# Ranking messages two double blocks of sources at a time in a two-layer graph network, with a fixed room per pair, places turned in the second layer, more gathers ahead and another order of the first loads

## The chip, the cores and the metric

The kernel runs on one core of a Trainium2 chip. The metric is device time in microseconds (us), the median of the runs shown. Engines: TensorE (PE) does matrix products and transposes, VectorE (DVE) element work, scans and reductions, ScalarE (ACT) activations and copies, GpSimd (POOL) here mostly issues indirect transfers, and SyncE (SP) issues plain transfers. ACT and POOL issue some plain transfers too.

## The reference

A graph with 6250 nodes of 128 features and 106250 edges, sorted by destination: each of 50000 random pairs in both directions, and a loop at every node. Every edge has one of four types and 64 attributes. Two layers, each behind a layernorm and a ReLU, each added to its input:

```
h = relu(layernorm(x))
x = x + layer0(h)
h = relu(layernorm(x))
x = x + layer1(h)
return x
```

`layer0` is an attention over edges for each type (8 heads of 16 channels): a logit from a score of the source and one of the destination, a softmax over the edges of the same destination and type, and the weighted sum of the source's transformed features. The four sums of a node go through a GELU and a matrix, and a second attention mixes them with the node's own features.

`layer1` takes each edge in both directions, passes (features of one end, features of the other end, attributes) through 320x256 weights, a leaky ReLU and 256x128 weights, and adds the result to the node at the end. So every edge gives one message to its destination and one to its source. A node network follows.

```
src_full = concatenate([src, dst]); dst_full = concatenate([dst, src])
msg = leaky_relu(concatenate([nf[src_full], nf[dst_full], ef_full]) @ We1) @ We2
red = segment_sum(msg, dst_full, num_segments=N)
out = leaky_relu(concatenate([nf, red]) @ Wn1) @ Wn2
```

## The kernel before

**Tiling.** 63 destinations are a block (`GB`), 126 a double block or unit (`DB`): 100 blocks (`NBK`) and 50 units (`NU`). The edges of a block lie one behind the other; each block gets 9 tiles (`TB`) of 128 edges, starting at its first edge (`st0`). So there are 900 tile columns (`NT`). In another layout, used for work over all edges at once, edge number 832 p + j is element j of partition p (`J` = 832).

**Preparation (L193 to L433).** SP loads `src`, `dst`, types and the next destination of each edge. ACT issues 22 loads of `x` (L220, L222), then those of the weights (L230 to L241). `scores` (L238) forms attention scores from weights. The block starts are found (L291 to L336), and with them SP issues 100 loads of pieces of `e2` (source and type in one number, and destination) as rows into ten `ct` tiles (L347). Then a loop over the 50 units (L352) normalizes, transposes and multiplies, and stores for each node and type a row of the table `xt`, through POOL (L377), and its own terms through ACT (L374). Behind it ten turns (L384 to L393) transpose the `ct` tiles into index columns (`xi`, `dloc`), and a chain of eight steps makes `srci`, `inb` and `key` (L394 to L402). `skey` (L419 to L429) is the unit of each edge's source, in the layout of 832.

**First layer (L438 to L860).** 25 steps (`NS`) of four blocks, nine tiles each. A tile's `gather0` issues four indirect gathers of `xt` rows on POOL (the helper `gather`, L81) into one of 18 `xg` buffers, 17 tiles (`LA0`) ahead of its use. `masks`, `logits` and `soft` (four scans of 1152 columns with one operand in PSUM) belong to the next step and are spread over the tiles of the present one; `messages` (L581) multiplies gathered rows by the weights and sums them by PE; `nodes` (L621) finishes the step before and stores the table `abtab`, from which the second layer reads.

**The ranks.** The second layer writes each message for a source to DRAM (`m2d`) at a place, so that messages for the same source lie together. Edges are cut into five parts (`NPT`) of 27 partitions of the 832-layout; within a part the messages are ordered by the unit of the source. `count` (L718) compares `skey` with one unit number and sums, for each partition; 50 counts are called over the first four steps (`NCS`). `counted` (L723) sums them across partitions into starts (`base1`, and `st1` for the readers). `rank` (L760), 50 times, three a step from step 4 on, compares again, scans the 832 columns into running places, and copies those of the unit into `plc` by a predicated copy:

```
ts_(ind, skey, float(b), None, op0=ALU.is_equal)
scan(place, ind, zrow, base1[:, b:b + 1], op0=ALU.add, op1=ALU.add)
nc.vector.copy_predicated(plc, ind, place)
```

`plc` is stored to DRAM (L746), read back block by block by `place_load` (L774, 100 small loads on SP in the last steps), and transposed into the index columns `placei` by `place_turn` (L781). Edges that aren't a block's own get a place in a trash area behind the messages (`trash`).

**Second layer (L914 to L1075).** For each of 450 tile pairs: `gather_pair` (two indirect gathers of `abtab` rows on POOL, 3 pairs ahead, `AHEAD`, with `AHEAD + 2` buffers `ag`), two products into `z` (L1046), the sum with the gathered rows into `s` (L1048, DVE), a multiplication by 0.01 (L1049, ACT) and a maximum (L1050, DVE), then two indirect scatters to `m2d` at `placei` (L1054, POOL), and two products that add the destination's messages (L1064). `ready(u)` (L987) loads a unit's attributes, destinations and `rhs` rows through SP and makes its left sides. `windows(j)` (L935) reads back part j of `m2d` in 50 windows, at starts from `st1` (L942), and sums by source (L963, L964), beside the tiles of a later part; the last part's windows come behind all tiles, with `node_update` (L872).

**Order.** Each engine runs its instructions in the order in which the program's scheduler put them, which starts from the order of the calls; waits between engines come from the tiles and buffers. At the end, a counter of exceptions (`oddi`) decides whether a general path does all again; with these inputs it doesn't run.

Of the kernel before, what the change touches and what calls it, by code (L numbers as in the profile page):

```python
# [56 lines left out]
LA0 = 17  # L57
NCS = 4
# [16 lines left out]
MW = HID + 1  # L75
TRASH = 64 * P
AHEAD = 3
# [8 lines left out]
def kernel(ctx: ExitStack, tc: tile.TileContext, x, src, dst, ef, et, w_rel, a_src, a_dst,  # L86
# [27 lines left out]
    m2d = dram("m2d", (E + TRASH, MW))  # L114
# [69 lines left out]
    zrow = p0.tile([P, J], F32, name="zrow")  # L184
    base1 = p0.tile([P, NU], F32, name="base1")
# [4 lines left out]
    pcol = p0.tile([P, 3], F32, name="pcol")  # L190
    cnt = p0.tile([P, NU], F32, name="cnt")

    with ExitStack() as prep:  # L193
        cpool = prep.enter_context(tc.tile_pool(name="prep", bufs=1))
        wpool = prep.enter_context(tc.tile_pool(name="prep2", bufs=2))
        pp = prep.enter_context(tc.tile_pool(name="prepp", bufs=2, space=PSUM))

# [15 lines left out]
        for u0 in range(0, NU, 10):  # L213
            nc.gpsimd.memset(x_sb[:, u0:u0 + 10, :], 0.0)
            for q in range(2):
                n0 = u0 * DB + q * GB
                k = 10 if u0 + 10 < NU else 9
                xq = x[u0 * DB:(u0 + k) * DB, :].rearrange("(u q r) c -> q r u c", q=2, r=GB)[q]
                for r0, r1 in ((0, 48), (48, GB)):
                    nc.scalar.dma_start(x_sb[q * 64 + r0:q * 64 + r1, u0:u0 + k, :], xq[r0:r1])  # L220
        for h, n in halves(NU - 1):
            nc.scalar.dma_start(x_sb[h, NU - 1, :], x[n, :])  # L222


        wall = cpool.tile([P, R * XR + R * H + C + 2 * H], F32, name="wall")
        wx = wall[:, 0:R * XR].rearrange("p (r c) -> p r c", r=R)
        wd = wall[:, R * XR:R * XR + R * H].rearrange("p (r h) -> p r h", r=R)
        wso = wall[:, R * XR + R * H:]
        wr = cpool.tile([P, R, C], F32, name="wr")
        nc.scalar.dma_start(wr, w_rel.rearrange("r i o -> i r o"))  # L230
        nc.scalar.dma_start(wso[:, 0:C], w_self)
        nc.scalar.dma_start(wcx[:, 0:C], w_cross)
        nc.scalar.dma_start(brT, b_rel.rearrange("r c -> c r"))
        blb = cpool.tile([P, C], F32, name="blb")
        nc.scalar.dma_start(blb, b_l.partition_broadcast(P))
        tmp = cpool.tile([P, R * C], F32, name="tmp")

        def scores(o, w, a, r):  # L238

            ab = wpool.tile([P, R * C], F32, name="ab")  # L240
            nc.scalar.dma_start(ab[:, 0:r * C], a.partition_broadcast(P))  # L241
            tt(tmp[:, 0:r * C].rearrange("p (r c) -> p r c", r=r), w,
               ab[:, 0:r * C].rearrange("p (r c) -> p r c", r=r), op=ALU.mult)
            red(o, tmp[:, 0:r * C].rearrange("p (r h d) -> p r h d", r=r, d=D), axis=AX.X, op=ALU.add)

        nc.gpsimd.tensor_copy(wx[:, :, 0:C], wr)
        scores(wx[:, :, C:XR], wr, a_src.rearrange("r h d -> (r h d)"), R)
        scores(wd, wr, a_dst.rearrange("r h d -> (r h d)"), R)
        ws1 = wso[:, 0:C].rearrange("p (r c) -> p r c", r=1)
        scores(wso[:, C:C + H].unsqueeze(1), ws1, a_src_l.rearrange("h d -> (h d)"), 1)  # L250
        scores(wso[:, C + H:C + 2 * H].unsqueeze(1), ws1, a_dst_l.rearrange("h d -> (h d)"), 1)
        wc1 = wcx[:, 0:C].rearrange("p (r c) -> p r c", r=1)
        scores(wcx[:, C:C + H].unsqueeze(1), wc1, a_src_l.rearrange("h d -> (h d)"), 1)
# [97 lines left out]

        for u in range(NU):  # L352
            if u % 10 == 0:
# [9 lines left out]
            w = R * XR // 2  # L363
            for k in range(2):
                nc.tensor.matmul(ps[:, k, 0:w], hT, wall[:, k * w:(k + 1) * w], start=True, stop=True)
            nc.vector.tensor_copy(row.rearrange("p (a c) -> p a c", a=2), ps[:, :, 0:w])
# [14 lines left out]
        first = cpool.tile([P, NBK, TB], F32, name="first")  # L381
        nc.gpsimd.iota(first, [[GB, NBK], [0, TB]], base=0, channel_multiplier=0, allow_small_or_imprecise_dtypes=True)
# [1279 lines left out]
```

## Time and profile before

| | |
|---|---|
| median of 3 runs | 4176.27 us (4169.11, 4176.27, 4177.46) |
| the profiled execution | 4172.47 us, span from first to last instruction 4170.7 us |
| mean granted TensorE clock | 0.86 |
| PE matmul busy | 3111.7 us, 75% of the span, 11258 instructions |
| PE weight load busy | 1790.3 us, 43% |
| DVE busy | 2830.8 us, 68%, 5244 instructions |
| ACT busy | 1574.8 us, 38%, 2994 instructions |
| POOL busy | 2899.4 us, 70%, 2887 instructions |
| DMA | 754.26 MB, mean 181 GB/s |

How to read the lines that follow. A line of the costliest groups has the source line, engine, operation and tiles, the count, then busy us and mean ns of one, then the idle us of the engine just ahead of them and what ended most of it ("issue": nothing that the profile shows). A windows line has a stretch of the span, its length, and the busy us of each engine in it with the number of instructions, then the granted clock, the share of DMA time and GB/s. A timeline line has the start in us from the span's start, the duration, the engine (with a q: its issue of a transfer, with the time until it landed), line, operation and tiles, and in brackets the wait before it and what ended it. The gathers of both layers have line 81, that of the helper; they are told apart by the tiles `xg` and `ag`.

### The profile page before, as it was taken

To read this page: it belongs to the slowest core of one execution; us is meant where nothing else is said; L and a number is where in the kernel's file an instruction comes from. 1 tells how busy PE (TensorE), PEld (TensorE's weight loads), DVE (VectorE), ACT (ScalarE), POOL (GpSimd) and SP (SyncE) were. 2 spreads that over 40 slices of the span, in tenths; PEclk is the share of its full clock that TensorE was granted. 3 is DMA by queue.
4 is the path that set the end of the run, shared out by engine and by line. 5 is a ranking of instruction groups with operands and counts; after the bars stand their busy time and mean duration, and the time that the engine had idled before them with its cause. 6 is when DMAs were issued, how large, how long until landed. Compare 5 with 4: busy or idle time off the path is not lost. (4 is left out here: it accounts for less than half of the span.)

```text
span 4170.7 us, 43560 instructions
## 1 busy us (share of the span) xinstructions
PE 3111.7 (75%) x11258; PEld 1790.3 (43%) x11258; DVE 2830.8 (68%) x5244; ACT 1574.8 (38%) x2994; POOL 2899.4 (70%) x2887
## 2 busy tenths in 40 slices
PE   4558877777888855666678887688768787688888
PEld 3346555555666642222234443344324333244456
DVE  6767899999777744455556665566657666577755
ACT  2356666656666532222222332222222222222211
POOL 5777777777777506777777777777777777777700
PEclk9768878888888868788889898888989989899999
DMA  6645444445555417666578886788868888588754
GB/s 180 168 102 120 113 113 114 114 112 119 118 119 122 105 41 202 175 180 184 165 212 247 252 253 197 227 249 240 246 197 265 242 237 251 170 263 274 242 164 139
DMA packets 414703, 754.26 MB, mean 181 GB/s; under 512 B 182863, under 2 KB 249525, under 8 KB 414445
## 3 DMA queue, kind: packets, MB, share of 16 engines
q0 software_dynamic: 148800, 430.91, 35.6%
q1 hardware_dynamic: 230376, 288.41, 26.6%
q10 hardware_dynamic: 35268, 32.07, 2.7%
q8 instruction: 92, 1.51, 0.2%
q14 instruction: 167, 1.36, 0.1%
HBM read 586.43 MB, written 164.69 MB: 180 GB/s over the span
## 5 line engine op out<-in xcount | busy, mean ns | idle before, releaser
L81 POOL DMA_INDIRECT xg<-xt,xi x900 | 980.5, 1089 | 289.0 <-issue 237.8
L81 POOL DMA_INDIRECT ag<-abtab,srci x900 | 907.4, 1008 | 303.4 <-issue 203.0
L1054 POOL DMA_INDIRECT m2d<-s,placei x900 | 913.9, 1015 | 288.6 <-issue 213.7
L1046 PE MATMUL z<-rhs,lt 128*128 128x512 f32 x1800 | 1037.5, 703 | 0.6 <-ACT lt L1017 0.6
L1050 DVE TENSOR_TENSOR s<-s,z 128x1024 f32<-128x1024 f32 x450 | 548.3, 1220 | 560.9 <-ACT z L1049 559.1
L1064 PE MATMUL sums<-s,oh 128*64 128x256 f32 x1800 | 338.3, 459 | 486.5 <-DVE s L1050 485.5
L1048 DVE TENSOR_TENSOR s<-z,ag 128x1024 f32<-128x1024 f32 x450 | 549.5, 1221 | 189.5 <-PE z L1046 156.0
L1049 ACT ACTIVATE z<-s 128x1024 f32<-128x1024 f32 x450 | 461.0, 1024 | 389.1 <-DVE s L1048 388.6
L592 PE MATMUL acc<-oh,msg 128*128 128x256 f32 x1800 | 501.9, 421 | 71.1 <-DVE oh L591 51.4
L1046 PEld LDWEIGHTS z<-rhs,lt 128*128 128x128 f32 x1800 | 353.2, 216 | 449.3 <-issue 442.8
L1051 ACT COPY s<-srcf 128x2 f32<-128x2 f32 x450 | 86.9, 193 | 1207.4 <-DMA m2d<-s,placei 1193.4
L964 PE MATMUL sums<-mt,ohw 128*128 128x256 f32 x2024 | 528.1, 394 | 9.2 <-DVE ohw L963 9.2
L964 PEld LDWEIGHTS sums<-mt,ohw 128*128 128x128 f32 x2024 | 392.4, 200 | 202.8 <-issue 133.9
L592 PEld LDWEIGHTS acc<-oh,msg 128*128 128x128 f32 x1800 | 363.3, 212 | 164.3 <-DVE oh L591 74.0
L1064 PEld LDWEIGHTS sums<-s,oh 128*64 128x64 f32 x1800 | 98.8, 149 | 729.7 <-DVE s L1050 570.5
L591 DVE TENSOR_SCALAR oh<-iota,key 128x256 f32<-128x256 f32 x900 | 309.6, 365 | 93.0 <-PE acc L592 88.7
L599 ACT ACTIVATE junk<-dt,nthr 128x1152 bf16<-128x1152 f32 x250 | 313.8, 1255 | 17.2 <-DMA dt<-dtyp 12.3
L963 DVE TENSOR_SCALAR ohw<-col,at 128x128 f32<-128x128 f32 x1012 | 250.5, 299 | 19.5 <-PE sums L964 11.3
L584 DVE TENSOR_TENSOR msg<-xg,pt 128x512 f32<-128x512 f32 x225 | 148.6, 676 | 86.5 <-PE pt L577 81.3
L1013 PE MATMUL tp<-ident,fe 128*128 128x128 f32 x450 | 86.6, 299 | 138.1 <-ACT lt L1017 107.2
L1017 ACT COPY lt<-tp 64x384 f32<-64x384 f32 x300 | 141.7, 472 | 111.3 <-PE tp L1013 62.7
L1013 PEld LDWEIGHTS tp<-ident,fe 128*128 128x128 f32 x450 | 58.9, 151 | 212.3 <-ACT lt L1017 140.8
(276 smaller groups left out, 3467.0 us busy)
## 6 DMA issues: line engine op xcount, KB each, us to landing
mt<-m2d SPq DMA_DIRECT2D x156, 514.0 KB
db<-in_dst_dram SPq DMA_DIRECT2D x200, 288.0 KB
mt<-m2d SPq DMA_DIRECT2D x53, 642.5 KB
dt<-dtyp SPq DMA_DIRECT2D x100, 288.0 KB
fe<-in_edge_attr_dram SPq DMA_DIRECT2D x100, 288.0 KB
mt<-m2d SPq DMA_DIRECT2D x41, 385.5 KB
xg<-xt,xi POOLq DMA_INDIRECT x900
ag<-abtab,srci POOLq DMA_INDIRECT x900
```

What stands on the lines that cost most here:

```text
L81: nc.gpsimd.indirect_dma_start(out=o, out_offset=None, in_=table, in_offset=bass.IndirectOffsetOnAxis(ap=idx.bitcast(I32), axis=0))
L591: ts_(oh.rearrange("p t n -> p (t n)"), iota, key[:, k:k + 1], None, op0=ALU.is_equal)
L592: nc.tensor.matmul(acc[q // 2][:, :, q % 2, :], msg[:, q, :], oh, start=(i == 0 and q % 2 == 0), stop=(i == TB - 1), skip_group_check=True)
L599: nc.scalar.activation(junk, lanes[s]["dt"][v], AF.Sign, bias=nthr[:, u, t:t + 1], accum_out=g[:, v, t:t + 1])
L963: ts_(oh, col, at[:, i:i + 1], None, op0=ALU.is_equal)
L964: nc.tensor.matmul(sums, oh, mt[:, i, 0:HID], start=(i == 0), stop=(i == n - 1))
L1046: nc.tensor.matmul(z[:, q, :], lt[q][:, i * P:(i + 1) * P], rhs[(2 * u + q) % 4], start=True, stop=True)
L1048: tt(s[:, :, 0:2 * HID], z, ags.pop(n), op=ALU.add)
L1049: nc.scalar.mul(z, s[:, :, 0:2 * HID], 0.01)
L1050: tt(s[:, :, 0:2 * HID], s[:, :, 0:2 * HID], z, op=ALU.max)
L1054: st = nc.gpsimd.indirect_dma_start(out=m2d, out_offset=bass.IndirectOffsetOnAxis(ap=placei[:, k:k + 1], axis=0), in_=s[:, q, HID:HID + MW ...
L1064: nc.tensor.matmul(sums[q * 64:(q + 1) * 64, :], oh[:, q * TB + i, :], s[:, q, 0:HID], start=(i == 0), stop=(i == TB - 1))
```

## The change

- **Counts and ranks.** A scan serves two units, g standing for units 2g and 2g + 1. `skey` becomes the pair's number, and `sunit` (bf16) is 1 for the first unit and 2048 (`FIELD`) for the second. `count(g)` forms `own_` = (`skey` == g) * `sunit` with its sum, in one DVE instruction, 25 instead of 50; 14 (`NC0`) stand ahead of step 0, the others follow at the tiles of the first two steps, fixed in program order. `rank(g)`, 25 instead of 50, forms `own_` again, scans it with a starting value that holds two counters, 2048 apart, and copies under the predicate `own_`. `ranked()` behind the last rank takes the right field out and adds the pair's start.
- **Fixed room.** Each pair of a part has 1280 places (`ROOM`), so a pair's start doesn't depend on the pairs ahead of it; `m2d` gets `PLACES` = 160000 rows and the trash area. `counted` decodes the two counters, and tests that no pair exceeds its room.
- **Places in layer 2.** `place_load` and `place_turn` become `places(pool, bank, g)`, called in the second layer: group 0 ahead of `ready(0)`, the nine others at every fifth unit (loads at tile 1, turn at tile 8 of unit u with u % 5 == 2).
- **Gathers ahead.** `AHEAD` goes from 3 to 7, so `ag` has nine buffers for five.
- **First loads.** ACT issues the weights and attention vectors first, then the loads of `x` for units 0 to 19; those for the later units go to SP, behind the loads of `src`, `dst` and types. `scores` is formed right behind.
- **Columns and keys.** The ten column turns go into the last ten turns of the unit loop (`columns`), and the key chain moves behind the constants of the first layer. In `nodes`, one comparison (`va`) is fixed in program order.

```diff
+NC0 = 14
...
+FIELD = 2048.0
+ROOM = 1280.0
+PLACES = int(NPT * NU // 2 * ROOM)
...
-AHEAD = 3
+AHEAD = 7
...
-    m2d = dram("m2d", (E + TRASH, MW))
+    m2d = dram("m2d", (PLACES + TRASH, MW))
...
+        nc.scalar.dma_start(wr, w_rel.rearrange("r i o -> i r o"))
+        nc.scalar.dma_start(wso[:, 0:C], w_self)
+        nc.scalar.dma_start(wcx[:, 0:C], w_cross)
+        atts = []
+        for a in (a_src.rearrange("r h d -> (r h d)"), a_dst.rearrange("r h d -> (r h d)"),
+                  a_src_l.rearrange("h d -> (h d)"), a_dst_l.rearrange("h d -> (h d)")):
+            ab = cpool.tile([P, a.shape[0]], F32, name=f"ab{len(atts)}")
+            nc.scalar.dma_start(ab, a.partition_broadcast(P))
+            atts.append(ab)
+        def scores(o, w, ab, r):
+            tt(tmp[:, 0:r * C].rearrange("p (r c) -> p r c", r=r), w,
+               ab[:, 0:r * C].rearrange("p (r c) -> p r c", r=r), op=ALU.mult)
+            red(o, tmp[:, 0:r * C].rearrange("p (r h d) -> p r h d", r=r, d=D), axis=AX.X, op=ALU.add)
...
-                    nc.scalar.dma_start(x_sb[q * 64 + r0:q * 64 + r1, u0:u0 + k, :], xq[r0:r1])
+                    (nc.scalar if u0 < 20 else nc.sync).dma_start(x_sb[q * 64 + r0:q * 64 + r1, u0:u0 + k, :], xq[r0:r1])
...
+        def columns(g):
+            ct = cts[g]
+            ctf = wpool.tile([w, 2, P], F32, name="ctf")
+            nc.vector.tensor_copy(ctf, ct)
+            tp = pp.tile([P, 2, w], F32, name="tp")
+            for a in range(2):
+                nc.tensor.transpose(tp[:, a, :], ctf[:, a, :], ident[0:w, 0:w])
+            s = slice(g * w, (g + 1) * w)
+            nc.vector.tensor_copy(xi[:, s], tp[:, 0, :])
+            tt(dloc[:, s], tp[:, 1, :], first.rearrange("p b i -> p (b i)")[:, s], op=ALU.subtract)
         for u in range(NU):
+            if u >= NU - NBK // CG:
+                columns(u - NU + NBK // CG)
...
+        stt(rest, skey, -2.0 * DB, sf, op0=ALU.mult, op1=ALU.add)
+        ts_(rest, rest, float(DB), FIELD - 1.0, op0=ALU.is_ge, op1=ALU.mult)
+        ts_(sunit, rest, 1.0, None, op0=ALU.add)
...
+        ti = key.bitcast(I32)
...
-            tt(va, gt[:, :, 0:R].rearrange("p v t -> p t v"), gt[:, :, 1:R + 1].rearrange("p v t -> p t v"), op=ALU.is_gt)
+            c = tt(va, gt[:, :, 0:R].rearrange("p v t -> p t v"), gt[:, :, 1:R + 1].rearrange("p v t -> p t v"), op=ALU.is_gt)
+            tc.keep_in_program_order(c)
...
-        def count(b):
-            ind = wp.tile([P, J], U8, name="ind", bufs=1)
-            ts_(ind, skey, float(b), None, op0=ALU.is_equal, op1=ALU.add, accum_out=cnt[:, b:b + 1])
+        def count(g, pin=False):
+            own_ = wp.tile([P, J], F32, name="own_", bufs=1)
+            c = stt(own_, skey, float(g), sunit, op0=ALU.is_equal, op1=ALU.mult, accum_out=cnt2[:, g:g + 1])
+            if pin:
+                tc.keep_in_program_order(c)
...
+            ci = cp.tile([P, 2, NG], I32, name="ci")
+            nc.vector.tensor_copy(ci[:, 0, :], cnt2)
+            ts_(ci[:, 1, :], ci[:, 0, :], 11, None, op0=ALU.logical_shift_right)
+            ts_(ci[:, 0, :], ci[:, 0, :], int(FIELD) - 1, None, op0=ALU.bitwise_and)
+            nc.vector.tensor_copy(cnt, ci.rearrange("p t g -> p g t"))
...
+            tt(base1, before[:, :, 1], tots[:, :, 0], op=ALU.add)
+            stt(base1, base1, FIELD, before[:, :, 0], op0=ALU.mult, op1=ALU.add)
...
+            ts_(s1[:, :, 0], numb[:, 0:NG], ROOM, pcol[:, 1:2], op0=ALU.mult, op1=ALU.add)
...
-        def rank(b):
-            ind = wp.tile([P, J], U8, name="ind", bufs=1)
-            ts_(ind, skey, float(b), None, op0=ALU.is_equal)
+            ts_(odds, ps[:, 0:1], 0.0, None, op0=ALU.is_equal)
+            ts_(inb, inb, odds, None, op0=ALU.mult)
+        def rank(g):
+            own_ = wp.tile([P, J], F32, name="own_", bufs=1)
+            stt(own_, skey, float(g), sunit, op0=ALU.is_equal, op1=ALU.mult)
             place = wp.tile([P, J], F32, name="place", bufs=1)
-            scan(place, ind, zrow, base1[:, b:b + 1], op0=ALU.add, op1=ALU.add)
...
-        def place_load(g):
-            ct = wp.tile([CG * TB, P], F32, name="ctp", bufs=3)
-            regs = first_of(st0, g * CG, CG, E - CAP)
-            for k in range(CG):
-                nc.sync.dma_start(ct[k * TB:(k + 1) * TB], plcd[0, ds(regs[k], CAP)].rearrange("(i p) -> i p", p=P))
-            pcs[g] = ct
-        def place_turn(g):
-            w = CG * TB
-            s = slice(g * w, (g + 1) * w)
-            tp = pa.tile([P, 512], F32, name="ent")
-            nc.tensor.transpose(tp[:, 0:w], pcs.pop(g), ident[0:w, 0:w])
-            pf = wp.tile([P, w], F32, name="pf", bufs=1)
-            tt(pf, tp[:, 0:w], trash, op=ALU.subtract)
-            tt(pf, pf, inb[:, s], op=ALU.mult)
-            tt(placei[:, s], pf, trash, op=ALU.add)
+            scan(place, own_, own_, base1[:, g:g + 1], op0=ALU.add, op1=ALU.max)
+            nc.vector.copy_predicated(plc, own_.bitcast(I32), place)
+        def ranked():
+            lo = wp.tile([P, J], F32, name="place", bufs=1)
+            hi = wp.tile([P, J], F32, name="own_", bufs=1)
+            lo, hi, pi = lo.bitcast(I32), hi.bitcast(I32), plc.bitcast(I32)
+            nc.vector.tensor_copy(lo, plc)
+            ts_(hi, lo, 11, None, op0=ALU.logical_shift_right)
+            ts_(lo, lo, int(FIELD) - 1, None, op0=ALU.bitwise_and)
+            ts_(pi, sunit, 1.0, None, op0=ALU.is_gt)
+            nc.vector.copy_predicated(lo, pi, hi)
+            stt(plc, skey, ROOM, lo, op0=ALU.mult, op1=ALU.add)
+            ts_(plc, plc, pcol[:, 1:2], 0.0, op0=ALU.add, op1=ALU.max)
+            ts_(plc, plc, PLACES - 1.0, None, op0=ALU.min)
+            nc.sync.dma_start(plcd[0].rearrange("(p j) -> p j", j=J), plc)
+        rank_at = [(s, i) for s in range(NCS, NS) for i in ((0, 5) if s % 2 else (0,))]
...
+        for b in range(NC0):
+            count(b)
...
-                if s < NCS:
-                    for b in range(s * TB + i, NU, NCS * TB):
-                        count(b)
-                elif s == NCS and i == 0:
+                g = NC0 + s * TB + i
+                if g < NU // 2:
+                    count(g, True)
+                if (s, i) == (NCS, 0):
                     counted()
-                if s >= NCS and i % 3 == 0:
-                    b = (s - NCS) * 3 + i // 3
-                    if b < NU:
-                        rank(b)
-                    if b == NU - 1:
-                        nc.sync.dma_start(plcd[0].rearrange("(p j) -> p j", j=J), plc)
-                g = (s - NS + 1) * 3 + NBK // CG + (i - 3) // 2
-                if 0 <= g < NBK // CG and i in (3, 5, 7):
-                    place_load(g)
+                if (s, i) in rank_at[:NU // 2]:
+                    rank(rank_at.index((s, i)))
+                    if rank_at.index((s, i)) == NU // 2 - 1:
+                        ranked()
...
+        def places(pool, bank, g):
+            w = CG * TB
+            s = slice(g * w, (g + 1) * w)
+            ct = pool.tile([w, P], F32, name="ctp", bufs=1)
+            regs = first_of(st0, g * CG, CG, E - CAP)
+            for k in range(CG):
+                nc.sync.dma_start(ct[k * TB:(k + 1) * TB], plcd[0, ds(regs[k], CAP)].rearrange("(i p) -> i p", p=P))
+            yield
+            tp = bank()[:, 0:w]
+            nc.tensor.transpose(tp, ct, ident[0:w, 0:w])
+            pf = pool.tile([P, w], F32, name="pf", bufs=1)
+            tt(pf, tp, trash, op=ALU.subtract)
+            tt(pf, pf, inb[:, s], op=ALU.mult)
+            tt(placei[:, s], pf, trash, op=ALU.add)
...
             for n in range(AHEAD):
                 gather_pair(n)
+            for _ in places(wp, bank, 0):
+                pass
             for _ in ready(0):
                 pass
...
+                more = u % 5 == 2 and 2 * u + 6 < NBK
+                plcs = places(wp, bank, (2 * u + 6) // CG) if more else iter(())
...
+                    if i in (1, TB - 1):
+                        next(plcs, None)
```

## The prediction

> **What bounds the kernel now.** First the costliest groups of the page: three groups of indirect transfers on GpSimd (POOL), 900 each.
>
> ```profile
> L81 POOL DMA_INDIRECT xg<-xt,xi x900 | 980.5, 1089 | 289.0 <-issue 237.8
> L81 POOL DMA_INDIRECT ag<-abtab,srci x900 | 907.4, 1008 | 303.4 <-issue 203.0
> L1054 POOL DMA_INDIRECT m2d<-s,placei x900 | 913.9, 1015 | 288.6 <-issue 213.7
> ```
>
> The reader is to see that idle time before them is almost all "issue", about 0.3 us for each: POOL goes from one to the next. In layer 1 they run from 164.2 to 1433.4 us, in layer 2 from 1557.1 to 3970.2; only 164 us ahead, 124 between and 200 behind are not theirs. So a change counts where it starts POOL earlier, shortens its hole or quickens its pace.
>
> Second the windows of layer 1, cut where the ranks (L763 to L766) begin and end:
>
> ```profile
> core 0: us, PE busy (x) PEld busy (x) DVE busy (x) ACT busy (x) POOL busy (x), PEclk, DMA share, GB/s
> 164.10:451.20 287.10, 186.10 (x735) 127.43 (x736) 212.26 (x436) 152.68 (x273) 218.76 (x217) 0.71 0.51 117
> 451.20:1047.50 596.30, 465.94 (x1925) 329.08 (x1924) 555.27 (x1065) 369.00 (x660) 470.80 (x396) 0.82 0.48 112
> 1047.50:1434.00 386.50, 320.73 (x1365) 239.04 (x1364) 290.16 (x664) 257.14 (x465) 290.89 (x288) 0.84 0.50 118
> ```
>
> POOL's instructions here are the gathers: 287.1/217 = 1.32 us each, then 1.51, then 1.34. While ranks run, DVE is 93% busy and a gather costs 0.17 us more; 396 x 0.17 = 68 us is what ranking costs today. Third, the groups of DVE with what it consists of, and two rows of the timeline that show how:
>
> ```profile
> L765 DVE TENSOR_TENSOR_SCAN place<-ind,base,zrow 128x832 f32<-128x832 uint8 x50 | 97.2, 1944 | 0.6
> ...
> L766 DVE COPY_PREDICATED plc<-ind,place 128x832 f32<-128x832 uint8 x50 | 54.2, 1084 | 0.6
> L721 DVE TENSOR_SCALAR_CACHE_REDUCE ind<-skey 128x832 uint8<-128x832 f32 x50 | 50.9, 1018 | 1.3
> ...
> L763 DVE TENSOR_SCALAR ind<-skey 128x832 uint8<-128x832 f32 x50 | 30.1, 602 | 0.4
> ```
>
> ```profile
> 635.00 1.94 DVE L765 TENSOR_TENSOR_SCAN place<-ind,base,zrow 128x832 f32<-128x832 uint8 x1
> 635.21 2.49 POOL L81 DMA_INDIRECT xg<-xt,xi  x1 [0.31 <-issue]
> ```
>
> A gather that meets this scan takes 2.49 us; the median gather takes 0.952. Scans that read one operand from PSUM (L552 to L563, 2.54 us each) leave gathers at that median. So DVE work with two SBUF inputs costs POOL time: 68 us over 50 ranks is 1.36 us a rank, 0.45 us per us of its 3.03 us of two-input work (scan and predicated copy).
>
> Fourth, the timeline of the front:
>
> ```profile
> 10.56 30.17 ACTq L220 DMA_DIRECT2D x_sb<-in_x_dram  x16
> ...
> 47.86 1.27 ACT L148 ACTIVATE sq<-h_sb 128x1280 f32<-128x1280 f32 x1
> ...
> 59.70 0.71 DVE L366 COPY row<-ps 128x544 f32<-128x544 f32 x1
> ...
> 161.72 0.35 POOL L445 IOTA iota<- 128x256 f32 x1 [8.15 <-DVE key L400]
> ...
> 164.16 1.05 POOL L81 DMA_INDIRECT xg<-xt,xi  x1 [0.25 <-issue]
> ```
>
> ACT issues 22 loads of x before its first arithmetic; the first row follows at 59.7, the last at 151.4, and the first gather waits a further 13 us for columns and keys.
>
> **The change, part by part**, against the profiled execution: 4172.5 us (span 4170.7 and 1.8 around it), 3.8 under the median of 4176.3.
>
> Front. ACT keeps 8 of the 22 x loads, behind 8 weight loads: 8 x 1.61 to 1.89 and some 10 x 0.44 make it free at about 20 us. DVE is late next: its run of preparations ended at 36.9; the score instructions move into it (4.4 us by L242 and L244) and one memset leaves (0.75), so 40.5; reduction, reciprocal and product of the first layernorm add 3.2, and from there to the first row copy it took 3.3 before (56.4 to 59.7): 47 instead of 59.7. The 50 units keep their 91.7 us. The column turns took 7.1 us in a row (150.3 to 157.4); among the last ten units DVE has room (0.72 of 1.83 us a unit) but PE and the two tp banks are shared, so I book half, 3.5. In the new order four key instructions (2.2) stand ahead of the last row: 144.4, if the columns are there. SP is passed by 14 x loads (some 25 us), so e2's stores go from 19 to about 42, and the 100 column loads, queued also behind two late lacks stores (after six rows, 47 + 11), start near 60 instead of 36.6. They took 81 us (36.6 to 117.7; 0.81 each, group g after 8.1 more), so group 0 is there near 70 and group 9 near 143, while the unit loop wants them at 47 + 40 x 1.83 = 120 and 137. The cover of 50 us for group 0 is gone at group 8, and the last turn waits some 6 us; of that the 2.2 of key work may lie in the wait: last row near 148.5. Store, landing and small POOL work 5: first gather at 153.5, **-10**. Bounds: -18 if the loads go quicker with the x loads done, and +5 if they start at 75: every us that they slip, all gathers slip.
>
> Counts. Fifty at 1.02 (and 0.08 to read) ran from 166 to 221; the first softmax scan (221.85) waited for its ninth tile (es copied at 217.67), so removing 25 gains nothing. No row shows the new form (two inputs with a sum); the plain two-input one of 900 columns takes 1.09, which gives about 1.02 for 832. The old count read one SBUF input, the new one two: 25 x 1.02 x 0.45 = **+11.5**; bounds 0 (like L721) and 25.5 (POOL held throughout).
>
> The Trainium skill, "SBUF — State Buffer", section "Who interferes with whom", says that an accumulating tensor_scalar leaves GpSimd alone, while two SBUF inputs on DVE shut out a GpSimd instruction that reads SBUF for the whole instruction. The trace agrees in kind (the gather at 635.21) but the mean loss is 0.45 and not 1; by the rule taken whole, counts would cost 25.5 and ranks 101.
>
> Ranks. 25 instead of 50, each now a two-input compare (about 1.02 for 0.60), scan 1.94 and copy 1.08: 4.04 x 0.45 = 1.82 us each, 45.5 against 68: **-22.5**. Bounds: 1.36 each, -34; every us lost, 101, +33. The instruction order puts them between tiles 39 and 98, 3.8 a step, as dense as today's 4.2 and over half as long. The decoding afterwards (8 instructions, 6 us, two of them with two inputs) and the longer counted step (a dozen at 0.2): **+2**, bounds 0 and 8.
>
> End of layer 1. Thirty small DVE steps, ten transposes and 100 place loads go. From 1433 to 1557 the path is the last two steps' logits, scans, messages and nodes; DVE idled at each place step there. **-1** (0 to -4). The pinned compare waited 8.8 us once, with a scan 0.8 us behind it: 0.
>
> Start of layer 2:
>
> ```profile
> 1569.38 0.95 POOL L81 DMA_INDIRECT ag<-abtab,srci  x1 [0.30 <-issue]
> ...
> 1582.90 1.23 DVE L1048 TENSOR_TENSOR s<-z,ag 128x1024 f32<-128x1024 f32 x1 [3.91 <-PE z L1046]
> ...
> 1584.40 1.41 POOL L81 DMA_INDIRECT ag<-abtab,srci  x1 [14.07 <-DVE s L1048]
> ```
>
> POOL makes 10 gathers, then waits 14 us for the first add to free a buffer. With nine buffers it makes 18: 8 x 1.26 = 10 us of that is used. But ten place loads now stand first on SP, ahead of fe, db and rhs that the add needs: 11.78/20 = 0.59 each, 5.9 us. Net **-4**; +6 if more gathers in flight slow db's landing too (11 us already), -10 if the loads hide.
>
> Layer 2. Of 2413 us POOL really waits about 25 beyond its cadence. AHEAD moves the wait of a gather, but the scatter behind it in the same queue still waits for s: **-2** (0 to -14). Nine more place groups: 5.9 us of SP each, one transpose, three DVE steps of 0.25, per 240 us; SP's window loads are two windows early and hide them: **+1**, 10 without that cover. The tail keeps its 200 us.
>
> Sum: -10 + 11.5 - 22.5 + 2 - 1 - 4 - 2 + 1 = -25, so 4147.5 for the profiled execution, and 3.8 more beside the median: about **4151**.
>
> **Rivals.** (1) Slower: two-input DVE work holds POOL wholly. New two-input work is 25 x 1.02 + 25 x 4.04 + 2.1 = 129 us; at a loss of 1 it costs 129 instead of 68, less 16 of the other terms: +45, 4221. It decides from (68 + 16)/129 = 0.65 upward; 0.45 is measured, on ranks spread as densely. For it: the 2.49 us gather. Chance 0.14. (2) Only a part comes: column loads that start 10 us later still eat the front; -15, 4161. Chance 0.22. (3) No change: the pace is set by the message steps, which run 17 to 18 tiles behind the gathers, as far as buffers allow, and new waits in SP's queue eat the rest; 4176. Against it: these steps also took 54 us with ranks and 48 without. Chance 0.09. The forecast has 0.55.
>
> **The numbers.** 0.2% is 8.4 us, about what a measurement can tell from no change. Forecast and (2) lie below 4168: faster 0.77; (3) same 0.09; slower 0.14. The range goes from -62 (ranks -34, counts 0, front -18, layer 2 -10) at 4114 to 4178, which takes in (2) and (3).
>
> **What would show it.** First row near 47, the last column load near 143 and the first gather near 153 us; gathers at about 1.5 us for some seven steps instead of twelve, 1.34 after; layer 2's first hole near 10 us; gathers and scatters at 1.33 as now. Wrong: a first gather after 164, counts under which gathers take 1.6, or scatters that wait for placei.

## The result, and the profile after

The changed kernel takes 4135.4 us (median of 4 runs, 4131.7 to 4145.1) beside 4174.7 for the kernel before (4 runs): a ratio of 0.991, 95% interval 0.990 to 0.993. The forecast was 4151, in a range from 4114 to 4178. Sign and range held; the sum was 12 us too small in the profiled executions (25 forecast, 37.5 measured: 4172.5 to 4135.0), and it was not made of the terms that the forecast gave it. Runs 5 to 12 below were taken where every kernel, the one before too, took about 20% longer; their times are compared only within their own sets.

Columns of the table: us of the profiled executions. The stages are cut at the first and last gather or scatter of each layer on POOL:

| stage | before | after | change | forecast |
|---|---|---|---|---|
| until the first gather | 164.2 | 154.9 | -9.2 | -10 |
| gathers of layer 1, first to last | 1269.2 | 1263.0 | -6.2 | -9 |
| from there to the first gather of layer 2 | 123.8 | 99.1 | -24.7 | -1 |
| layer 2, first gather to last scatter | 2413.1 | 2416.3 | +3.2 | -5 |
| behind it | 200.5 | 200.0 | -0.5 | 0 |

The page of after, its groups of indirect transfers:

```profile
L85 POOL DMA_INDIRECT xg<-xt,xi x900 | 961.6, 1068 | 301.7 <-issue 244.2
L1104 POOL DMA_INDIRECT m2d<-s,placei x900 | 915.6, 1017 | 297.9 <-issue 217.4
L85 POOL DMA_INDIRECT ag<-abtab,srci x900 | 905.6, 1006 | 297.3 <-issue 204.6
```

Only the gathers of layer 1 became shorter (1089 to 1068 ns); the other two groups are as before. The windows of layer 1, with the ranks in the second (columns as in the windows of before):

```profile
154.90:391.00 236.10, 140.03 (x536) 93.87 (x536) 146.86 (x301) 117.30 (x206) 179.29 (x176) 0.70 0.51 116
391.00:826.30 435.30, 351.77 (x1432) 248.05 (x1431) 385.46 (x760) 270.02 (x489) 340.47 (x293) 0.82 0.47 112
826.30:1418.00 591.70, 494.07 (x2078) 364.80 (x2077) 436.62 (x986) 416.85 (x723) 441.87 (x432) 0.82 0.52 122
```

236.1/176 = 1.34 us for a gather with the counts, 435.3/293 = 1.49 with the ranks, and then 591.7/432 = 1.37, where the kernel before had 1.34. The second window takes in 60 us ahead of the first rank's scan, which starts at 451.6; from there on 249 gathers take 374.7 us, 1.50 each, for 396 at 1.51 before. So a gather beside the ranks costs what it did, and about seven steps of 36 gathers have it instead of eleven (forecast: seven for twelve); but the stretch behind the ranks became slower.

The front of after, three views put together (SP's, DVE's and POOL's rows of the timeline):

```profile
63.04 80.62 SPq L356 DMA_DIRECT2D ct<-e  x100
...
45.94 0.72 DVE L392 COPY row<-ps 128x544 f32<-128x544 f32 x1 [0.19 <-PE ps L391]
...
139.78 0.72 DVE L392 COPY row<-ps 128x544 f32<-128x544 f32 x1 [1.17 <-DMA xt<-row]
145.92 0.29 DVE L367 CAST ctf<-ct 90x256 f32<-90x256 int32 x1 [5.42 <-DMA ct<-e]
...
149.61 0.72 DVE L392 COPY row<-ps 128x544 f32<-128x544 f32 x1 [0.19 <-PE ps L391]
...
154.94 1.53 POOL L85 DMA_INDIRECT xg<-xt,xi  x1 [0.33 <-DMA t<-turnd]
```

The 13.8 us that the first row gains (59.7 to 45.9) are not all kept: the column loads on SP end at 143.7, DVE waits 5.4 us for the last of them, and the last row stands behind that turn.

The stretch between the layers. The timeline of before, PE's rows and then DVE's:

```profile
1453.20 5.78 PE L592 MATMUL acc<-oh,msg 128*128 128x256 f32 x26
1463.60 0.33 PE L521 MATMUL lg<-ne,pen 16*128 16x384 bf16 x1
...
1483.15 2.56 DVE L552 TENSOR_TENSOR_SCAN f<-km,l 128x1152 f32<-128x1152 f32 x1 [0.62 <-ACT l L534]
```

and of after:

```profile
1425.92 0.33 PE L535 MATMUL lg<-ne,pen 16*128 16x384 bf16 x1
1427.75 2.76 PE L606 MATMUL acc<-oh,msg 128*128 128x256 f32 x12
1430.99 1.03 PE L606 MATMUL acc<-oh,msg 128*128 128x256 f32 x4
1431.95 0.33 PE L535 MATMUL lg<-ne,pen 16*128 16x384 bf16 x1
...
1441.11 2.55 DVE L566 TENSOR_TENSOR_SCAN f<-km,l 128x1152 f32<-128x1152 f32 x1
```

`lg<-ne` opens a third of the logits of the last step, `acc<-oh,msg` are the products of the step before it. In the kernel before, the last step's logits stand on PE behind all products of step 23; in the changed kernel they stand among them, as in all earlier steps of both kernels. The first scan of the last step starts 72.1 us behind that of step 23 in the one (1411.06 to 1483.15) and 47.8 in the other (1393.36 to 1441.11).

The start of layer 2 in after, SP's, DVE's and POOL's rows:

```profile
1517.09 6.28 SPq L959 DMA_DIRECT2D ctp<-plcd  x8
...
1533.29 0.82 DVE L1051 TENSOR_SCALAR lt<-db,swap 64x1152 f32<-64x1152 int32 x1 [5.70 <-DMA db<-in_dst_dram]
1540.85 0.81 DVE L1051 TENSOR_SCALAR lt<-db,swap 64x1152 f32<-64x1152 int32 x1 [6.75 <-DMA db<-in_dst_dram]
...
1546.23 0.95 POOL L85 DMA_INDIRECT ag<-abtab,srci  x1 [5.71 <-DVE s L1098]
```

The 14.07 us hole is 5.7 us now, with 18 gathers ahead of it; the place loads go first on SP, and DVE waits for `db` behind them.

### The profile page after: what moved, and what is told of

The parts are those of the page before. It is cut to its first block, busy times and chain, and to the rows that moved or that the text cites. A ratio compares the mean times of both kernels' runs of the same rounds, so it can differ in the third digit from the quotient of the medians.

```text
span 4133.3 us, 43383 instructions
## 1 busy us (share of the span) xinstructions
PE 3116.2 (75%) x11258; PEld 1791.8 (43%) x11258; DVE 2739.6 (66%) x5139; ACT 1604.5 (39%) x3014; POOL 2883.5 (70%) x2887
## 3 DMA queue, kind: packets, MB, share of 16 engines
q0 software_dynamic: 148800, 430.91, 35.6%
q8 instruction: 92, 1.51, 0.2%
## 5 line engine op out<-in xcount | busy, mean ns | idle before, releaser
L85 POOL DMA_INDIRECT xg<-xt,xi x900 | 961.6, 1068 | 301.7 <-issue 244.2
L554 PE MATMUL km<-t,turn 8*128 8x512 bf16 x150 | 45.8, 421 | 136.3 <-DVE l L577 44.3
```

Source lines behind the costliest of these rows:

```text
L85: nc.gpsimd.indirect_dma_start(out=o, out_offset=None, in_=table, in_offset=bass.IndirectOffsetOnAxis(ap=idx.bitcast(I32), axis=0))
```

## The experiments

Each edit is shown against the changed kernel where nothing else is said, with "..." where lines are left out. Lane loads are the loads of a step's edges through SP (`loads(s)`: `t`, `db`, `ne`, `dt`), two steps ahead of their use; the gap is the time from the last gather of layer 1 to the first of layer 2.

Theories: **A**, the 24.7 us between the layers come from where the last step's logits stand in the instruction order. **B**, the place steps themselves cost them, by their waits. **C**, the comparison fixed in program order brought them. Of the slower pace behind the ranks, which the first two runs brought up: **D**, the order of DVE's instructions in the steady step; **E**, the removal of the places does it in another way.

**1. Places back in layer 1.** Places alone are undone; everything else stays changed.

```diff
+            yield
+            g = (s - NS) * 3 + NBK // CG
+            for k in range(3):
+                if 0 <= g + k < NBK // CG:
+                    place_turn(g + k)
...
+                g = (s - NS + 1) * 3 + NBK // CG + (i - 3) // 2
+                if 0 <= g < NBK // CG and i in (3, 5, 7):
+                    place_load(g)
                 if i == 5 and s + 2 < NS:
                     loads(s + 2)
...
-            for _ in places(wp, bank, 0):
-                pass
```

> The changed kernel, with the place loads and place turns back in the last steps of layer 1, at the places where the kernel before has them; all else stays changed. In the instruction order the logits of step 24 then stand behind all products of step 23 on PE, as before; in the changed kernel they stand among them. Theory A (order: the 24.7 us that the gap between the last gather of layer 1 and the first of layer 2 lost, 123.8 to 99.1, come from that order): the gap returns to about 124, messages of step 23 to 24 take 73 us instead of 48, and the time is about 4155 (25 more, less some 5 that the place loads no longer take at the start of layer 2). Theory B (the place steps themselves cost it, by their waits on DVE and PE): the same here. Theory C (the comparison fixed in program order brought it): the gap stays near 99, 4135.

**2. The same, with the place loads behind the lane loads** (against run 1).

```diff
-                g = (s - NS + 1) * 3 + NBK // CG + (i - 3) // 2
-                if 0 <= g < NBK // CG and i in (3, 5, 7):
-                    place_load(g)
                 if i == 5 and s + 2 < NS:
                     loads(s + 2)
+                g = (s - NS + 1) * 3 + NBK // CG + i - 6
+                if 0 <= g < NBK // CG and i >= 6:
+                    place_load(g)
```

> As the run before, but each step's place loads stand behind the lane loads of the step after next in the program (tiles 6, 7, 8 instead of 3, 5, 7). The same 100 loads and ten turns are in layer 1; in the instruction order the logits of step 24 are back among the products of step 23. Theory A (order): the gap is near 100 to 105 although all place steps are there, and the time 4130 to 4140. Theory B (the place steps themselves): the gap is 118 or more, about 4150. Theory C (the fixed comparison): 99 here too, and no difference from the run before.

**3. Without the fixed comparison.**

```diff
-            tc.keep_in_program_order(c)
```

> The changed kernel without the fixed program order of the comparison in the node steps. Theory A (order of the logits): the gap stays near 99, since the logits of step 24 stay where they are. Theory C: it grows by 9 or more, the wait for the tally that was seen before the first scan of the last step. Of the pace: message steps 12 to 23 took 49.3 us in the changed kernel and 48.4 in the rank-free steps before; if the fixed comparison costs that, they fall to 48.4 and the time by about 10, to 4125; if not, 4135.

**4. Three gathers ahead.**

```diff
-AHEAD = 7
+AHEAD = 3
```

> The changed kernel with AHEAD = 3 and five buffers, as before. Forecast's theory (the longer lead fills the hole at the start of layer 2 and costs nothing later): the first four units take 6 us longer (111.8 against 105.3 for 72 transfers of the kernel before and this one), so 4141. Rival (the lead is given back at the end: the last two units took 109.9 us with seven ahead and 101.4 with three, as only scatters are left there, which wait for sums): start 6 longer, end 8 shorter, so 4133, no difference that can be told.

Measured, beside runs of the kernel before on the same chip (its median 4182.6; the changed kernel beside 4174.7, from above). The last four columns are us of the profiled executions, the last of them from the first message product of step 23 to that of step 24:

| kernel | median | ratio, 95% interval | layer 1 | gap | layer 2 | messages of step 23 to 24 |
|---|---|---|---|---|---|---|
| after (from above) | 4135.4 | 0.9913 (0.9896 to 0.9929) | 1263.0 | 99.1 | 2416.3 | 47.9 |
| 1, places back | 4125.3 | 0.9871 (0.9852 to 0.9891) | 1241.3 | 116.0 | 2405.5 | 70.4 |
| 2, places back, loads late | 4114.7 | 0.9838 (0.9824 to 0.9852) | 1244.6 | 104.1 | 2408.1 | 49.3 |
| 3, comparison not fixed | 4145.1 | 0.9905 (0.9888 to 0.9923) | 1266.6 | 99.4 | 2423.2 | 45.8 |
| 4, AHEAD = 3 | 4134.8 | 0.9884 (0.9867 to 0.9901) | 1265.4 | 102.8 | 2411.8 | 48.8 |

Between the layers it counts where the place loads stand, and B, the place work itself, falls. Runs 1 and 2 do the same 100 loads and ten turns in layer 1 and differ in three lines; the gap is 116.0 and 104.1, and the step to the last one 70.4 and 49.3 us. Of the 21 us, run 1 gets 9 back behind that step (46.0 us from there to the first gather of layer 2, 54.7 in run 2), so its gap stays below the 124 that were expected, and 12 us of the gap are shown to hang on these lines. The places' own work is about the 5 us between run 2 and after. PE's first logits of the last step in run 1, and DVE's first scan behind them:

```profile
1414.33 5.34 PE L606 MATMUL acc<-oh,msg 128*128 128x256 f32 x24
1425.73 0.49 PE L535 MATMUL lg<-ne,pen 16*128 16x384 bf16 x1
...
1444.12 2.56 DVE L566 TENSOR_TENSOR_SCAN f<-km,l 128x1152 f32<-128x1152 f32 x1 [8.86 <-ACT l L548]
```

and the same scan in run 2, in its usual place:

```profile
1426.31 2.55 DVE L566 TENSOR_TENSOR_SCAN f<-km,l 128x1152 f32<-128x1152 f32 x1
```

SP in run 1 and then in run 2, the place loads `ctp` and the last `db` of the last step's lane loads:

```profile
1385.28 11.77 SPq L829 DMA_DIRECT2D ctp<-plcd  x20
...
1406.32 0.47 SPq L512 DMA_DIRECT2D db<-in_dst_dram  x1
```

```profile
1381.54 0.48 SPq L512 DMA_DIRECT2D db<-in_dst_dram  x1
...
1394.14 17.03 SPq L829 DMA_DIRECT2D ctp<-plcd  x30
```

So the change gained here not by moving work to layer 2 but because its place loads no longer stand on SP ahead of the last step's lane loads; the instruction order has the logits behind all products where they do. Whether that order alone cost the time, as A says, or loads that came late isn't separated: with the order the last `db` load moved too. It was issued 9.7 us behind the first product of step 23 in run 1 (1396.61) and 21.4 ahead of it in run 2 (1402.93); 8.6 behind it in the kernel before and 19.7 ahead in after. The first logits follow it by 13 to 19 us in all four, so most of their shift is already in the loads. C falls with run 3: the gap stays at 99.4 without the fixed comparison.

What nobody expected is the other column: with the places back, layer 1 takes 22 us less. POOL's own rows of the waits, from 880 to 1360 us, in after and then in run 2 (total, times, longest):

```profile
POOL xg L85 <- issue: 99.7, 278, 3.3
```

```profile
POOL xg L85 <- issue: 88.7, 291, 0.3
```

In run 2 POOL never waits longer than the 0.3 us between two gathers: the gathers set the pace (47.9 us a step is 36 x 1.33). In after it stops seven times, for 1.8 to 3.3 us, some 15 us in all; the profile names no releaser, and a free buffer is the likely one, since a message step takes 49.5 us on average of steps 12 to 22. The work of the step is the same in both. The order of DVE isn't. In short from the instruction order of step 17 (M message product, o one-hot, b m r statistics and root of the node step, F A L the scans and their products, h the normalized rows, T a mask; the first scan is the first F):

```
after:   ..bbmmomromrorMrorororrrorFhhAoFoTooooooALTF
run 2:   ..bbmomomromrMrororFrorArorFrohhoTAoLoooooTF
```

In after the first scan stands behind all ten r; in run 2 behind five of them. In step 17 it starts 25.7 us after the step's first message in after, and 24.5 in run 2; the last F, the share, starts at 42.2 and 41.0, and the next step's messages wait for it. Run 4, which has the order of after, has its pace (message steps 48.1 to 50.8 from 14 to 22); run 1 has the order of run 2 and a mean of 48.0 over steps 12 to 22. Run 3 alternates between two further orders, and between 48.5 and 50.4. The place of the first scan can't be all: it stands behind eight r in the kernel before from step 17 on, with steps of about 48.2 there, and behind eight in those steps of run 3 that take 50.4.

Run 4 also settles the gathers ahead. Counted by POOL's transfers, 36 a unit, the first four units take 207.8 us for 201.0 with seven, the last two 100.9 for 109.6. The end in after (waits on POOL from 3824 to 3935):

```profile
POOL m2d L1104 <- DVE s L1100: 12.1, 8, 2.8
...
POOL m2d L1104 <- DVE ohw L1006: 7.1, 7, 2.4
```

With seven ahead the last 20 transfers are scatters alone (12 with three), and they wait for sums, which DVE makes between the windows. What the start gains, the end gives back: no difference that the intervals can tell. The gain at the start is the lead itself: 82 of its 144 transfers are gathers, for 78 with three, and the 72nd scatter ends 224.5 us after the first gather with seven and 221.1 with three.

**5 to 8. The columns early; ranks twice; the kernel before with its loads late; five ahead.** In 5, the stores of `turnd`, `lacks` and `dtyp` go behind the column loads:

```diff
-            ne = wpool.tile([P, J], BF16, name="ne")
+            ne = cpool.tile([P, J], BF16, name=f"ne{r}")
...
             cts.append(ct)
+        for r in range(R):
+            nc.sync.dma_start(lacks[r].rearrange("(p j) -> p j", j=J), nes[r])
```

> The changed kernel with the stores of turnd, lacks and dtyp behind the 100 column loads on SP (four ne tiles instead of two, so that DVE needn't wait for them). Two effects are expected. Front: if the column loads set the end of the front (they ran from 63.0 to 143.7 and the last turn waited 5.4 us for them), they start near 39 and end near 120, the last turn doesn't wait, and the first gather is near 149 instead of 154.9; if the unit loop sets it, 154 to 155. Steps: in the instruction order of this kernel the steady steps of layer 1 have the order of DVE that the run with the places back had (first scan behind the second group of the node steps' small instructions), not that of the changed kernel (behind all of them, and behind two h). Theory D (the order of the steady step costs 1.5 us a step: message steps 12 to 22 took 49.5 us in the changed kernel and 47.9 with the places back): message steps near 47.9, gathers of layer 1 in 1243 us instead of 1263, and the time 4108. Theory E (the place steps' removal slows layer 1 in another way): 1263 as in the changed kernel, 4130.

In 6:

```diff
                     rank(rank_at.index((s, i)))
+                    rank(rank_at.index((s, i)))
```

> The changed kernel with each of the 25 ranks done twice (same result). Added: 25 times 4.05 us of two-input work on DVE, spread to 7 a step. By the forecast's 0.45 us of POOL lost for each us, +45; by the 0.36 that gathers overlapped by ranks show in the changed kernel (36.6 us for 101.3), +36; held wholly, +101; bound by DVE itself (ranked steps then hold about 51 us of DVE work), more than 45, with gathers that wait for messages. The steady steps behind the ranks have the other order of DVE here too, so by theory D 10 to 15 of it come back: 4156 to 4170.

In 7, the edit of run 2 in the kernel before:

```diff
-                if 0 <= g < NBK // CG and i in (3, 5, 7):
...
+                if 0 <= g < NBK // CG and i >= 6:
```

> The kernel before with one thing moved: the place loads stand behind the lane loads of the step after next (tiles 6, 7, 8 instead of 3, 5, 7). In the instruction order the logits of step 24 are then among the products of step 23, as in the changed kernel. Theory A: messages of step 23 to 24 fall from 72.8 to about 50 us and the gap from 123.8 to about 102. Theory D: the steady steps of this kernel alternate between two orders, as in the run without the fixed comparison (48.5 and 50.4 there, 48.2 in the kernel before), so up to 1.2 us in each of the 7 rank-free steps is lost: about 4160 in all. If the place work itself was the cause: 4175, no difference.

In 8, run 5 with

```diff
-AHEAD = 7
+AHEAD = 5
```

> As the run with the columns early, with AHEAD = 5 and seven buffers. With three ahead the first four units took 6.8 us longer than with seven and the last two 8.7 shorter, so each is paid at one end. Theory F (a trade at both ends): half of each, within 3 us of the run with seven. If the start needs fewer than seven but the end pays only above five: 3 to 6 us faster.

**9 and 10. All counts ahead of step 0; the best parts together.** In 9:

```diff
-NC0 = 14
+NC0 = 25
```

> The changed kernel with NC0 = 25 for 14: all counts stand ahead of step 0, and no work is added or taken. In the instruction order the steady steps of layer 1 then have the other order of DVE (the first scan behind the second group of the node steps' small instructions, as with the places back), the rest is the same. Theory D (the order of the steady step costs 1.5 us a step, since the scan chain and not the gathers then sets the pace): message steps 12 to 22 near 47.9 us instead of 49.5, gathers of layer 1 in 1243 to 1250 us instead of 1263, and the time 4115 to 4122. Theory E (layer 1 was quicker with the places back because of the places): 49.5 a step and 4135.

Run 10 has the edit of run 2, the stores of run 5 behind the column loads, and this; `NC0` stays 14:

```diff
-        rank_at = [(s, i) for s in range(NCS, NS) for i in ((0, 5) if s % 2 else (0,))]
...
+        rank_at = [(s, i) for s in range(NCS, NS) for i in ((1, 5) if s % 2 else (1,))]
```

> Places back in layer 1 with their loads behind the lane loads, the stores of turnd, lacks and dtyp behind the column loads, and the ranks one tile later where they stood at tile 0 (which keeps the quicker steady order; with tile 0 the order is the slower one). Against the run with the places back and late (4114.7): if the column loads set the end of the front, the first gather goes from 157.4 to about 149, and the time to about 4107; if the unit loop sets it, 4114.

**11 and 12. Run 9 twice more.**

> The changed kernel with NC0 = 25 for 14: all counts stand ahead of step 0, and no work is added or taken. The steady steps of layer 1 then have the order of DVE that the run with the places back had. In the set before this one every kernel, the one before included, took some 20% longer, with message steps of 75 us whatever their order, so it said nothing on this. Theory D (the order of the steady step costs 1.5 us a step, since the scan chain and not the gathers sets the pace): message steps 12 to 22 near 47.9 us instead of 49.5, gathers of layer 1 in 1243 to 1250 us instead of 1263, and the time 4115 to 4122. Theory E (layer 1 was quicker with the places back because of the places): 49.5 a step and 4135.

> Once more the changed kernel with NC0 = 25 for 14: all counts stand ahead of step 0, no work is added or taken, and the steady steps of layer 1 have the order of DVE that the run with the places back had. In the two sets before, every kernel took some 20% longer, so they said nothing on this. Theory D (the order of the steady step costs 1.5 us a step): message steps 12 to 22 near 47.9 us instead of 49.5, gathers of layer 1 in 1243 to 1250 us instead of 1263, and the time 4115 to 4122. Theory E (layer 1 was quicker with the places back because of the places): 49.5 a step and 4135.

In the sets of runs 5 to 12 the kernel before had medians of 5035 (5 to 8), 4978 (9 and 10), 5038 (11) and 4963 us (12). Ratios to the kernel before in the same set: 0.999 for run 5 (0.997 to 1.002), 0.992 for 6 (0.988 to 0.995), 1.004 for 7 (1.002 to 1.006), 1.000 for 8 (0.998 to 1.003), 0.999 for 9 (0.997 to 1.002), 1.007 for 10 (1.004 to 1.011), 0.998 for 11 (0.994 to 1.001), 1.002 for 12 (0.999 to 1.004). There message steps take about 75 us whatever the order (73 to 75 in steps 14 to 22 of run 9, 71 to 84 in run 6). The waits of run 9, from 900 to 1300 us, show another limit:

```profile
DVE oh L605 <- remote: 82.4, 20, 11.4
...
ACT l L546 <- remote: 44.8, 5, 11.1
```

The releaser "remote" is no instruction or transfer of this program that the profile shows. So theory D, that order alone does it, stays a reading of five traces; it wasn't shown by the run meant for it, and the time of the combined kernel beside run 2 is unknown.

Run 7 still bears on what lies between the layers. In it all three logits of the last step stand among the products, and the step from 23 to 24 takes 50.4 us, for 72.8 in the kernel before as profiled above. That kernel wasn't profiled in the same set, but in the other kernels of runs 5 to 12, in which no place load stands ahead of the lane loads either, this step takes 47.4 to 48.9, as it does in after. The gap of run 7 is 126.7 and not the 102 expected: its last gather ends 22 us ahead of the messages of step 23, for 2 in the kernel before.

The front can still be read in them, since it is the same there (first gather at 155.0 in run 9, 154.9 in after). Run 5, SP, DVE and POOL:

```profile
41.09 91.16 SPq L352 DMA_DIRECT2D ct<-e  x100
...
142.04 0.72 DVE L395 COPY row<-ps 128x544 f32<-128x544 f32 x1 [1.12 <-DMA xt<-row]
...
148.97 1.82 POOL L85 DMA_INDIRECT xg<-xt,xi  x1 [1.58 <-issue]
```

The loads start 22 us earlier, end at 132, no turn waits for them, and the first gather comes at 149.0. Runs 8 and 10 have the same stores; there a turn still waits some 3 us, and the first gather comes at 152.6 and 151.3, where the changed kernel and its variants without that edit have it between 154.6 and 157.4. So the columns did set the end of the front in after, and 2 to 8 us more are to be had.

The price of a rank can be read as well, from gathers that a rank's instructions overlap: in after 87 of them between 390 and 830 us, with a mean of 1458 ns, and 1038 for the 209 others, so 36.5 us lost for 101.3 us of such work, 0.36. In the same way 62.4 us for 151.4 in the kernel before, 0.41. Run 6, doubled, loses 45.7 for 202.8, and run 12, single, 23.6 for 101.4: 0.23 in both. Runs 9 and 11, single too, have about 25 and 18, so 0.17 to 0.25 in these four; twice the work cost about twice the loss.

Of the versions measured beside a kernel before of about 4180 us, run 2 is the quickest: 0.9838, with its whole interval below the changed kernel's. The places belong in layer 1, once their loads are out of the lane loads' way.

## Why the prediction was right, and where it was wrong

**Front: right, also in its reason.** First row at 45.9 (47 forecast), column loads from 63.0 to 143.7 (60 to 143), a wait of 5.4 us for the last (6), first gather at 154.9 (153.5). -9.2 for -10.

**Ranks: right.** A step is counted here as 36 gathers. With 48.2 us for a step without ranks in the kernel before, its steps 5 to 16 hold 646.5 - 12 x 48.2 = 68 us of excess, those of after (5 to 12) 428.9 - 8 x 48.2 = 43: -25 for the -22.5 and +2 of ranks and decoding. The mean loss that the forecast took from the trace of before was the right measure; the Trainium skill's rule in "SBUF — State Buffer", "Who interferes with whom", taken whole, would have given, as an estimate, 101 us of loss (25 x 4.04) for what cost 37.

**Counts: right sign, half the size.** Steps 0 to 4 took 242.5 us for 236.8: +5.7 for +11.5. The term at fault is the loss of 0.45 per us, which came from scans and predicated copies. The 28 gathers that overlap a count have a mean of 1187 ns, the 81 others until 300 us 976: 5.9 us lost for 25.2 us of counts, 0.23.

**End of layer 1: the step that failed.** The forecast read the 8.8 us wait before the last step's first comparison and the scan 0.8 us behind it, and put both at 0, and the whole stage at -1. It saw that DVE "idled at each place step there" and took the last two steps' logits as a fixed path; it left out what the place loads did on SP, ahead of the last step's lane loads. That path was 24 us longer than in other steps, with the logits behind the products; the interval from one first scan to the next, 72 us where the other steps show 48, would have told it, and the instruction orders of the two kernels showed where the logits had gone. Runs 1 and 2 put 21 us of the step, and 12 of the gap, on where the place loads stand; order and late loads aren't told apart, and the rest of the 24.7 isn't put down to a cause by a run.

**Pace behind the ranks: a missing term.** Steps 13 to 24 took 591.6 us for 12 x 48.2 = 578: +13. The forecast looked at the new order for ranks, counts and turns and took the steady step as unchanged. Rival 3 named the mechanism (the message steps set the pace), put it at all of layer 1 and gave it 0.09; by POOL's waits it holds for the half behind the ranks. Why the steps became longer stays open.

**Layer 2: a lead that is given back.** By POOL's transfers the first four units gained 7.6 us (208.6 to 201.0; -4 forecast), but the 72nd scatter came no earlier (224.5 us after the first gather, 221.6 before), so the gain was lead and no progress. The place loads ahead of `db` cost what was read from SP's rows: without them run 1 takes 194.5, 6.5 us less (5.9 forecast). The last two units took 109.6 for 101.1: the forecast had no term for these 8.5 us at the end. Nine more place groups beside the windows don't show: the middle took 2105.7 for 2103.3.

Rival 1, POOL held wholly, falls (0.36 measured, 0.65 needed). Rival 2's delay of the columns didn't come.

**The total: in part luck.** The 24 us that the forecast didn't see between the layers stand against 13 behind the ranks and 8 in layer 2 that it didn't see either; counts and ranks, put 6 and 4 us too dear, are most of the rest. Without the 13 and the 8 the time would be about 4114, the edge of the range; without the 24, about 4159. That the total came so near rests on errors that nearly cancel.

## What to carry to other kernels

Where a scheduler writes the instruction order, compare the order of the steady step and of the last step, not only the edited lines: steps of the same work differed by 1.5 us between two orders (that the order did it isn't shown), and three lines that changed places on SP's queue moved 21 us of a step and 12 of the gap. Measure each step's length from one marker (a first scan, a first message) to the next: a step that is 1.5 times as long as its neighbours, as the last one was here, is worth a look. A longer lead of gathers filled the start of the loop here and was paid at its end, where only the consumers are left.

## What the runs showed of the hardware

For each us of scans and predicated copies with two SBUF operands on DVE, overlapping gathers lost 0.41 us on POOL in the kernel before and 0.36 in the changed kernel; 0.17 to 0.25 in runs 6, 9, 11 and 12, where gathers stood further apart (about 75 us for 36 instead of 48). The counts, a comparison of two SBUF operands with a sum, cost 0.23 (5.9 us for 25.2).

Why a message step takes 75 us in run 9 stays open. The packets of the software queue took as long as in after (30.1% of 4949 us are 1490, 35.6% of 4133 are 1471), and the gathers too (1020 ns for 1068); the time went into waits that no instruction of the program ends, by the profile. The last step, behind the last gather, took 47.8 us there, as in after.
